# Four moves of vector and scalar work inside the steady step of a four-layer graph kernel

## The chip, the core and the metric

The kernel runs on one core of one Trainium2 chip. A core has five engines with a queue each: TensorE (PE, matmuls), VectorE (DVE, elementwise and reductions), ScalarE (ACT, activations and copies), GpSimd (POOL) and SyncE (SP, which here only issues DMAs). Each engine takes its own queue in order, and semaphores make it wait for another. The metric is device time in microseconds (us), lower is better; the time before is the median of three runs.

## The reference, cut to what matters

The input x is 128 graphs of 64 nodes with 512 features, in float32. Four layers follow one another, each with a residual and a layer norm:

- layer 0: a hypergraph convolution (512 to 1024 features, relu, layer norm over 1024, back to 512), `y + x`, then again `x + ...` and a layer norm;
- layer 1: a score per node, `exp(leaky(8 tanh(s/8)))` times the adjacency, normalised, applied to x and multiplied by `w`;
- layer 2: three graph convolutions, `relu(adj @ (x @ W1) + b1)`, `relu(adj @ (. @ W2) + b2)`, `adj @ (. @ W3) + b3`;
- layer 3: attention with 8 heads, whose probabilities get `LG * adj + LD * exp(-adj)` added under a mask, an output projection and a bias.

Two pieces of algebra matter below. The kernel folds layer 0's inner layer norm into W2: gamma scales W2's rows, and beta times W2 becomes a row `bw_bc` that is added to x, scaled by a column sum `cs` of the graph matrix. And x is doubled and gets b2 before W2's product is added, since layer 0 adds x twice.

## The kernel before, in words

**Tiling.** Two graphs fill the 128 partitions (a pair), four pairs are a group of 512 rows, and there are 16 groups. Every group goes through three parts: `a` (layers 0 and 1, `first_half`), `b` (layer 2 and the queries and keys of layer 3, the first part of `second_half`) and `t` (the rest of layer 3). Step s works on part `a` of group s, part `b` of group s-1 and part `t` of group s-2 at once; steps 2 to 15 are the steady ones, and have one order of pieces (`order`, L1285). Step 1, step 16 and what follows have orders of their own.

**Products.** A 512x512x512 product (`multiply`, L520) is made of seven products of halves instead of eight, in the order B11, T1, T2, B21, T3, B22, T4. They accumulate in three PSUM tiles: `a` takes B11, then T2, T3 and T4 on top; `b` takes T1, then B22; `c` takes B21. Between them the running values are evicted: u1 after B11, u5 after T1, u2 after T2 (`snap`, L525), and the four results after B21, T3, B22 and T4. So T2 can't start before u1 is out of `a`, T3 not before u2, T4 not before the result after T3. The activations' side needs four sums of quarters (`Left.sums`, L488, four VectorE additions); the weights' sums lie in DRAM and are streamed by SP through a ring of 20 tiles. The first and second product of layer 0 are called W1a and W1b here (hidden columns 0 to 511 and 512 to 1023), the third W2 (twice as deep); layer 2's are l2a, l2b and l2c.

**What sets the order of the work.** In the steady steps the program's text gives only a priority: a scheduler at build time places each instruction on its engine's queue. `behind(key)` (L475) keeps instructions behind a named one, which is the eviction after B22 of product `key`. The order on the chip is that of the built program and doesn't change with the data. In a steady step of the program before, it is:

- PE: ... layer 2's aggregation `gt_l` of group s-1, W1a, l2a, W1b with the transposes of the probabilities in it, the attention product `pv` of group s-2, l2b with half of layer 0's `gt_l0h`, the other half, W2 with layer 2's `gth` in it, l2c, ...
- PE twice takes a product apart: W1a's B21 (tile `c_l0w`) runs half before T2 and half after it, and W1b's first product runs a quarter before l2a's T4 and the rest after it.
- DVE, around W1a: the sums of layer 2 (`s_l`, `aT_l`; `left.sums()` at L993), then u1, u5, u2 and the results of W1a, then `doubled` (L791) and `constant` (L797, the column-sum scalings), then the results of l2a.
- ACT: the relu of W1b's two halves of rows (L702; the second is a 128x1024 activation behind the last eviction of W1b), then four copies of the attention product out of PSUM (`aT_oT`, L1275), with a table load and two square roots among them, then u1 of l2b.
- DVE, between l2b's last eviction and W2's first: x plus b3 (`gb3_bc`, L1008), the masks of layer 3 (`prepare_masks`, L654), eight sums for W2.
- SP: the masks of a later group (`mj`, `mr`) are reloaded into buffers that `prepare_masks` has just read, between the weights of l2c.

Of the kernel before, what the change touches and what calls it, by code (L numbers as in the profile page):

```python
# [8 lines left out]
FP = mybir.dt.float32  # L9
U8 = mybir.dt.uint8  # L10
AF = mybir.ActivationFunctionType
# [3 lines left out]
P = 128  # L15
C = 64
D = 512
DH = 1024
HEADS = 8
G = 4  # L20
T = G * P
KD = D // P
Q = 256
# [18 lines left out]
def kernel(  # L42
# [31 lines left out]
    NGRP = NPAIR // G  # L74
# [8 lines left out]
    grp = ctx.enter_context(tc.tile_pool(name="grp", bufs=2))  # L83
# [52 lines left out]
    ten, vec, act = Engine(nc.tensor, PE), Engine(nc.vector, DVE), Engine(nc.scalar, ACT)  # L136
# [288 lines left out]
    def bcast(t, n):  # L425

        return t.unsqueeze(2).to_broadcast([P, n, C])

    def row2(t, c0):

        return t[:, c0 : c0 + Q].unsqueeze(1).to_broadcast([P, 2, Q])
# [38 lines left out]
            act.copy(o[:, :, :, g, :], ps[g])  # L470


    last_add = {}

    def behind(key):  # L475
        return tc.issue_after(last_add[key]) if key in last_add else nullcontext()
# [43 lines left out]
    def multiply(lefts, wt_q, dst, key, flipped=False, res=None, stops=(3,)):  # L520


        acc = [ps_acc.tile([P, 2, Q], FP, name=f"{n}_{key}", tag="acc") for n in "ab"]

        def snap(ps, m, n, what):  # L525
            t = work.tile([P, 2, Q], FP, name=f"{what}_{key}", tag="w")
            if res is None:
                act.copy(t, ps)
            else:
                vec.tensor_add(t, ps, res(m, n))  # L530
            return t

        pa, pc = acc
        product(pa, lefts, wt_q, B11, True, False, flipped)
        s1 = snap(pa, 0, 0, "u1")
        if 1 in stops:
            yield
        product(pc, lefts, wt_q, T1, True, False, flipped)
        s5 = snap(pc, 1, 1, "u5")
        if 2 in stops:  # L540
            yield
        product(pa, lefts, wt_q, T2, False, False, flipped)
        s2 = snap(pa, 0, 1, "u2")
        if 3 in stops:
            yield
        pb = ps_acc.tile([P, 2, Q], FP, name=f"c_{key}", tag="acc")
        product(pb, lefts, wt_q, B21, True, True, flipped)
        vec.tensor_add(dst(0, 0), pb, s1)
        if 4 in stops:
            yield  # L550
        product(pa, lefts, wt_q, T3, False, False, flipped)
        vec.tensor_add(dst(1, 1), pa, s5)  # L552
        if 5 in stops:
            yield
        product(pc, lefts, wt_q, B22, False, True, flipped)
        last_add[key] = vec.tensor_add(dst(0, 1), pc, s2).ins  # L556
        if 6 in stops:
            yield
        product(pa, lefts, wt_q, T4, False, True, flipped)
        if res is None:  # L560
            act.copy(dst(1, 0), pa)
        else:
            vec.tensor_add(dst(1, 0), pa, res(1, 0))
# [9 lines left out]
    def turned(t):  # L573

        return lambda m, n: t[:, 2 * n : 2 * n + 2, m * Q : (m + 1) * Q]
# [78 lines left out]
    def prepare_masks(g):  # L654
        q = g["q"]
        mj, mr = g["mj"], g["mr"]

        neg = grp.tile([P, 2, 2, C], FP, name=f"neg_{q}", tag="neg", bufs=1)
        n3 = neg.rearrange("p a g j -> p (a g) j")
        vec.tensor_mul(  # L660
            n3, mj.rearrange("p a g j -> p (a g) j"), bcast(mi[:, q * G : (q + 1) * G], G)
        )
        vec.tensor_scalar(neg, neg, BIG, BIG, ALU.mult, ALU.subtract)

        m2 = grp.tile([P, G, C], FP, name=f"m2_{q}", tag="m2", bufs=1)
        vec.tensor_mul(m2, mr, bcast(mcol[:, q * G : (q + 1) * G], G))
        adt = grp.tile([P, G, C], FP, name=f"adt_{q}", tag="adt", bufs=1)
        act.activation(adt, g["atc"], AF.Exp, scale=-1.0)
        if LD != LA:
            vec.tensor_scalar_mul(adt, adt, LD / LA)  # L670
        vec.scalar_tensor_tensor(adt, g["atc"], LG / LA, adt, ALU.mult, ALU.add)
        vec.tensor_mul(adt, adt, m2)
        g["neg"], g["adt"] = neg, adt


    def first_half(g):
        q, xg = g["q"], g["x"]
        pair = lambda p: xg[:, p, :]

        left = Left(f"l0_{q}")  # L680
# [4 lines left out]
        h = [big.tile([P, 2, DH], FP, name=f"h_{q}_{m}", tag="big") for m in range(2)]  # L685
        for n in range(2):
            for i, _ in enumerate(multiply(
                [left], (w_1[n], q),
                lambda m, k: h[m][:, :, n * D + k * Q : n * D + (k + 1) * Q],
                f"l0w1{n}_{q}",  # L690
                res=lambda m, k: row2(b1_bc, n * D + k * Q),
                stops=((2, 4), (2, 3))[n] if q == 1 else (3,),
            )):
                yield f"w1{'ab'[n]}{i + 1}"
            yield "w1" + "ab"[n]

            if n == 0:
                st = small.tile([P, G, 2, 6], FP, name=f"sth_{q}", tag="sth", bufs=2)
            with behind(f"l0w1{n}_{q}"):
                for m in range(2):  # L700
                    hn = h[m][:, :, n * D : (n + 1) * D]
                    act.activation(hn, hn, AF.Relu)  # L702
                    for p in range(2):
                        vec.bn_stats(st[:, 2 * m + p, n, :], hn[:, p, :])
            if n == 0:
                if q > 1:
                    with behind(f"l0w10_{q}"):
                        doubled(g)
                        constant(g)
                yield "resid"  # L710
        for m in range(2):
            mv = small.tile([P, 2, 2], FP, name=f"mvh_{q}_{m}", tag="mvh")
# [9 lines left out]
        for duo in range(2):  # L722
            for u in range(2):
                graph_T(
                    lambda p: h[p // 2][:, p % 2, u * D : (u + 1) * D], g["sm"], lefts[u].t, duo, f"l0h{u}_{q}"
                )
            if duo == 0:
                yield "c2a"
        for left in lefts:
            left.sums()  # L730
        yield "c2b"
# [21 lines left out]
        t = grp.tile([P, G, C], FP, name=f"t_{q}", tag="t", bufs=1)  # L753
# [16 lines left out]
        left = Left(f"l1_{q}")  # L770
# [26 lines left out]
    def constant(g):  # L797
        for p in range(G):
            vec.scalar_tensor_tensor(
                g["x"][:, p, :], bw_bc, g["cs"][:, p : p + 1], g["x"][:, p, :], ALU.mult, ALU.add  # L800
            )
# [184 lines left out]
    def second_half(g):  # L986
        q, xg = g["q"], g["x"]
        pair = lambda p: xg[:, p, :]

        left = Left(f"l2_{q}")  # L990
        for duo in range(2):
            graph_T(pair, g["atc"], left.t, duo, f"l2_{q}")
        left.sums()  # L993
        yield "gt"
        h1 = Left(f"h1_{q}")
        for _ in multiply([left], (w_g[0], q), turned(h1.t), f"l2a_{q}", flipped=True):
            yield "l2a1"
# [5 lines left out]
        for _ in multiply([h1], (w_g[1], q), nat(g2), f"l2b_{q}"):  # L1003
            yield "l2b1"
        yield "l2b"
        with behind(f"l2b_{q}"):
            for p in range(G):
                vec.tensor_add(xg[:, p, :], xg[:, p, :], gb3_bc)  # L1008
            prepare_masks(g)
        yield "gb3"  # L1010


# [1 line left out]
        for c2 in range(2):  # L1014
            ps = [ps_gt.tile([P, 2, G, C], FP, name=f"gth2_{q}_{c2}_{h}", tag="gt") for h in range(2)]
            for c in range(2):
                for p in range(G):
                    for f in range(2):
                        for h in range(2):
                            rows, c0 = slice(h * C, (h + 1) * C), (2 * c2 + c) * P + f * C  # L1020
                            ten.matmul(  # L1021
                                ps[h][f * C : (f + 1) * C, c, p, :],
                                g2[rows, p, c0 : c0 + C], g["atc"][rows, p, :], start=True, stop=True,
                            )
            for c in range(2):
                k = 2 * c2 + c
                o = h2.t[:, k, :].rearrange("p (d h t) -> p d h t", d=2, h=2)
                for h in range(2):
                    act.activation(  # L1029
                        o[:, :, h, :], ps[h][:, c].rearrange("p (d a) i -> p d (a i)", d=2),  # L1030
                        AF.Relu, bias=gb2_col[:, k : k + 1],
                    )
        h2.sums()
        yield "gh"
        g3 = big.tile([P, G, D], FP, name=f"g3_{q}", tag="big")
# [3 lines left out]
        for duo in range(2):  # L1039
            ps = [ps_gt.tile([P, D], FP, name=f"agg_{q}_{duo}_{p}", tag="gt") for p in range(2)]  # L1040
# [14 lines left out]
        left = Left(f"xT_{q}")  # L1055

        for duo in range(2):
            ps = [ps_gt.tile([P, KD, 2, C], FP, name=f"xtp_{q}_{duo}_{h}", tag="gt") for h in range(2)]
# [40 lines left out]
        left = Left(f"oT_{q}")  # L1099
# [204 lines left out]
    for what in start:  # L1304
        who, dot, name = what.partition(".")
# [7 lines left out]
    for step in range(1, NGRP + 2):  # L1313
        for what in orders.get(step, order):
            who, dot, name = what.partition(".")
            key = (who, step - lag[who], name) if dot else (what, step + 1, None)
# [24 lines left out]
    for n, (who, q, name) in enumerate(todo):  # L1341
# [28 lines left out]
        elif who == "rest":  # L1370
            with in_turn(SP, POOL):
# [8 lines left out]
                gb3_bc = load_row(gb3, D, "gb3_bc")  # L1380
# [66 lines left out]
```

## Time and profile before

| what | value |
|---|---|
| median of 3 runs | 2797.4 us (2797.36 to 2798.42) |
| the profiled execution | 2797.61 us, its span 2795.8 us, TensorE clock 1.00 |
| PE busy | 2769.4 us (99%) |
| DVE busy | 2000.2 us (72%) |
| ACT busy | 818.3 us (29%) |
| one steady step, from one `dot` to the next | 171.77 us |

The span runs from the first to the last instruction. PE is the engine without room; the others have idle time that costs nothing as long as PE doesn't wait for them. Matmuls are pipelined, and one that is held up looks busy while it is held: the distance between the starts of successive groups tells more than their busy time.

### The profile page before, as it was taken

How to read it: one execution, taken by the hardware profiler on the slowest of the kernel's cores; microseconds unless marked ns; L12 is line 12 of the kernel's file. 1: busy time of each engine (PE TensorE's matmuls, PEld its weight loads, DVE VectorE, ACT ScalarE, POOL GpSimd, SP SyncE). 2: the span in 40 equal slices, each digit the busy share in tenths (PEclk: the TensorE clock that was granted, in tenths of full speed). 3: DMA queues.
4: the chain of work that ended last, by engine and by line, in shares of the span. 5: the costliest groups of instructions: out<-in, count | busy, mean ns of one | idle time of the engine just before them, and what ended most of it. 6: DMA issues, size and time to landing. Idle time of an engine off the chain costs nothing.

```text
span 2795.8 us, 67769 instructions
## 1 busy us (share of the span) xinstructions
PE 2769.4 (99%) x28870; PEld 2362.2 (84%) x28870; DVE 2000.2 (72%) x3858; ACT 818.3 (29%) x1469; POOL 38.1 (1%) x72
## 2 busy tenths in 40 slices
PE   9999999999999999999999999999999999999998
PEld 7878888888888888888888888888888888888887
DVE  6768687676776767767677676767767677676766
ACT  3222323232232223323223222332322323232232
POOL 2000000000000000000000000000000000000000
PEclk9999999999999999999999999999999999999999
DMA  8444455454544545445454454544545455454541
GB/s 255 162 136 145 129 158 145 133 163 130 166 130 140 161 132 166 122 141 165 124 168 130 139 161 136 155 130 143 162 127 163 129 148 152 126 163 127 154 122 61
DMA packets 309389, 405.15 MB, mean 145 GB/s; under 512 B 57409, under 2 KB 185185, under 8 KB 309089
## 3 DMA queue, kind: packets, MB, share of 16 engines
q1 hardware_dynamic: 304112, 385.05, 46.5%
q0 software_dynamic: 4976, 15.76, 1.5%
q8 instruction: 229, 3.75, 0.5%
q14 instruction: 72, 0.58, 0.1%
HBM read 369.78 MB, written 30.93 MB: 143 GB/s over the span
## 4 chain that ended last, share of the span: by engine, by line
PE 86%; DVE 7%; issue 4%; ACT 1%; DMA 1%; POOL 0%; SPq 0%; DVEq 0%; POOLq 0%
PE a_l0w L513 13%; PE b_l0w L513 7%; PE a_l2b L513 4%; PE a_q L513 4%; PE a_k L513 4%; PE a_v L513 4%; PE c_l0w L513 4%; PE a_l2a L513 4%; PE a_l1w L513 4%; PE gt_l L462 3%; PE a_wo L513 3%; PE a_l2c L513 2%; PE gt_l0h L462 2%; PE b_l1w L513 2%; PE b_l2b L513 2%
## 5 line engine op out<-in xcount | busy, mean ns | idle before, releaser
L513 PE MATMUL a_l0w<-w2w,aT_l0h 128*128 128x256 f32 x720 | 164.3, 381 | 0.0
L444 DVE BATCH_NORM_STATS2 st_l<-x 128x6 f32<-128x512 f32 x244 | 157.4, 671 | 0.1
L513 PEld LDWEIGHTS a_l0w<-w2w,aT_l0h 128*128 128x128 f32 x720 | 135.6, 190 | 18.8
L702 ACT ACTIVATE h<-h 128x1024 f32<-128x1024 f32 x58 | 61.3, 1057 | 216.6 <-DVE h L556 195.0
L448 DVE TENSOR_SCALAR x<-x,mv_l,rs_l 128x512 f32<-128x512 f32 x244 | 117.9, 540 | 1.8
L470 ACT COPY aT_l<-gt_l 128x512 f32<-128x512 f32 x176 | 90.4, 600 | 71.6 <-PE gt_l L462 71.5
L513 PE MATMUL b_l0w<-w2w,s_l0h 128*128 128x256 f32 x480 | 108.5, 379 | 0.0
L513 PEld LDWEIGHTS b_l0w<-w2w,s_l0h 128*128 128x128 f32 x480 | 90.1, 190 | 13.5
L1029 ACT ACTIVATE aT_h<-gth,gb_col 128x256 f32<-128x256 f32 x128 | 48.4, 489 | 159.0 <-PE gth L1021 159.0
L435 ACT ACTIVATE rs_l<-mv_l,eps_t 128x4 f32<-128x4 f32 (+1 forms) x64 | 19.0, 297 | 253.7 <-DVE mv_l L445 241.9
L513 PE MATMUL a_l2b<-gwbw,aT_h 128*128 128x256 f32 x360 | 86.6, 383 | 5.4 <-ACT aT_oT L1275 5.4
L513 PE MATMUL a_q<-aT_xT,wqw 128*128 128x256 f32 x360 | 86.6, 383 | 0.7 <-ACT aT_xT L1068 0.7
L513 PE MATMUL a_l2a<-aT_l,gwaw 128*128 128x256 f32 x360 | 86.5, 383 | 0.0
L513 PE MATMUL a_l2c<-gwcw,aT_h 128*128 128x256 f32 x360 | 85.3, 380 | 0.6 <-DVE g L552 0.6
L513 PE MATMUL a_l1w<-ww,aT_l 128*128 128x256 f32 x360 | 85.1, 379 | 0.0
L513 PE MATMUL a_k<-aT_xT,wkw 128*128 128x256 f32 x360 | 85.0, 379 | 0.0
L513 PE MATMUL a_l0w<-w1aw,aT_l 128*128 128x256 f32 x336 | 82.3, 388 | 0.0
L513 PE MATMUL a_l0w<-w1bw,aT_l 128*128 128x256 f32 x336 | 81.7, 379 | 0.0
L530 DVE TENSOR_TENSOR u_l0w<-a_l0w,b_bc 128x512 f32<-128x512 f32 x56 | 38.4, 686 | 59.8 <-PE a_l0w L513 59.8
L513 PE MATMUL a_v<-wvw,aT_xT 128*128 128x256 f32 x336 | 80.8, 383 | 0.0
L513 PEld LDWEIGHTS a_l2b<-gwbw,aT_h 128*128 128x128 f32 x360 | 67.2, 190 | 15.9 <-ACT aT_oT L1275 7.4
L513 PE MATMUL a_wo<-wow,aT_oT 128*128 128x256 f32 x336 | 79.5, 379 | 0.1
(531 smaller groups left out, 6471.1 us busy)
## 6 DMA issues: line engine op xcount, KB each, us to landing
w2w<-w2k SPq DMA_DIRECT2D x210, 256.0 KB, 2.7
x<-in_x_dram SPq DMA_DIRECT2D x15, 1024.0 KB, 6.7
w1aw<-w1ak SPq DMA_DIRECT2D x60, 256.0 KB, 2.7
w1bw<-w1bk SPq DMA_DIRECT2D x60, 256.0 KB, 2.6
ww<-wk SPq DMA_DIRECT2D x60, 256.0 KB, 2.8
gwaw<-gwak SPq DMA_DIRECT2D x60, 256.0 KB, 3.6
gwbw<-gwbk SPq DMA_DIRECT2D x60, 256.0 KB, 2.7
gwcw<-gwck SPq DMA_DIRECT2D x60, 256.0 KB, 2.7
```

The costliest lines, as they stand in the source:

```text
L435: act.activation(rs[:, at], mv[:, at, 1], AF.Sqrt, bias=eps_t)
L444: vec.bn_stats(st, xg[:, p, :])
L448: vec.tensor_scalar(xg[:, p, :], xg[:, p, :], mv[:, p, 0:1], rs[:, p : p + 1], ALU.subtract, ALU.mult)
L462: ten.matmul(ps[g][f * C : (f + 1) * C, c, p, :], src(2 * duo + p)[rows, c0 : c0 + C], mat[rows, 2 * duo + p, :], start=True, stop=True,)
L470: act.copy(o[:, :, :, g, :], ps[g])
L513: ten.matmul(acc[:, blk, :], lhsT, rhs, start=(first and blk == 0 and i == 0), stop=(last and i == n_k - 1), skip_group_check=True,)
L530: vec.tensor_add(t, ps, res(m, n))
L702: act.activation(hn, hn, AF.Relu)
L1029: act.activation(o[:, :, h, :], ps[h][:, c].rearrange("p (d a) i -> p d (a i)", d=2), AF.Relu, bias=gb2_col[:, k : k + 1],)
```

## The change

It moves four things of the steady step and leaves the arithmetic as it is:

1. layer 2's sums go from before W1a's u1 to behind W1a's u2 ("the third eviction");
2. `constant` goes from behind W1a to behind l2b's eviction after B22 of the group before;
3. the addition of b3 and `prepare_masks` go from behind l2b to behind W2's u2;
4. the last relu of W1b is issued in two halves of columns, the half that T3 completes first.

To be able to name u1, u5 and u2, `snap` now notes each in `last_add`. Groups 0 and 15 keep the old place of points 1 and 3 (`alone`), and point 2 holds for groups above 1.

```diff
         def snap(ps, m, n, what):
             t = work.tile([P, 2, Q], FP, name=f"{what}_{key}", tag="w")
-            if res is None:
-                act.copy(t, ps)
-            else:
-                vec.tensor_add(t, ps, res(m, n))
+            last_add[f"{key}.{what}"] = (act.copy(t, ps) if res is None else vec.tensor_add(t, ps, res(m, n))).ins
             return t
...
-        adt = grp.tile([P, G, C], FP, name=f"adt_{q}", tag="adt", bufs=1)
-        act.activation(adt, g["atc"], AF.Exp, scale=-1.0)
+        adt = g["adt"]
...
+    def shifted(g, key):
+
+        with behind(key):
+            for p in range(G):
+                vec.tensor_add(g["x"][:, p, :], g["x"][:, p, :], gb3_bc)
+            prepare_masks(g)
...
                     hn = h[m][:, :, n * D : (n + 1) * D]
+                    if n == 1 and m == 1:
+
+                        act.activation(hn[:, :, Q:], hn[:, :, Q:], AF.Relu)
+                        hn = hn[:, :, :Q]
                     act.activation(hn, hn, AF.Relu)
                     for p in range(2):
-                        vec.bn_stats(st[:, 2 * m + p, n, :], hn[:, p, :])
+                        vec.bn_stats(st[:, 2 * m + p, n, :], h[m][:, p, n * D : (n + 1) * D])
...
                         doubled(g)
-                        constant(g)
...
             if duo == 0:
                 yield "c2a"
+        if q > 1:
+            with behind(f"l2b_{q - 1}"):
+                constant(g)
...
-        left.sums()
+        alone = q == 0 or q == NGRP - 1
+        if alone:
+            left.sums()
         yield "gt"
+        if not alone:
+            with behind(f"l0w10_{q + 1}.u2"):
+                left.sums()
...
-        with behind(f"l2b_{q}"):
-            for p in range(G):
-                vec.tensor_add(xg[:, p, :], xg[:, p, :], gb3_bc)
-            prepare_masks(g)
+        adt = grp.tile([P, G, C], FP, name=f"adt_{q}", tag="adt", bufs=1)
+        act.activation(adt, g["atc"], AF.Exp, scale=-1.0)
+        g["adt"] = adt
+        if alone:
+            shifted(g, f"l2b_{q}")
         yield "gb3"
...
+        if not alone:
+            shifted(g, f"l0w2_{q + 1}.u2")
         h2.sums()
         yield "gh"
```

In the built program the queues of steps 2 to 15 change as follows, and nowhere else except for the relu of step 1. PE: W1a's B21 is in one piece behind T2, and W1b's first product in one piece behind l2a's T4; all else stands as before. DVE: two of layer 2's sums stand behind u2, the result after B21 follows, then the other two; the four `constant` instructions and the nine of b3 and masks change places as described. ACT: one instruction more a step, in the order right half of the second row block, first row block, left half of the second. SP: the four mask loads stand behind the fifth of the seven weight tiles of the output projection, where they stood between the weights of l2c. POOL has no change.

More of the change, by code (lines that the diff above doesn't have):

```diff
@@ L672, in prepare_masks @@
         vec.tensor_mul(adt, adt, m2)
-        g["neg"], g["adt"] = neg, adt
+        g["neg"] = neg
+    def shifted(g, key):
[3 more added lines that the diff above has]
+            prepare_masks(g)
     def first_half(g):
```

## The prediction

> **What bounds the kernel now.** The page first: its head, part 1.
>
> ```profile
> span 2795.8 us, 67769 instructions
> PE 2769.4 (99%) x28870; PEld 2362.2 (84%) x28870; DVE 2000.2 (72%) x3858; ACT 818.3 (29%) x1469; POOL 38.1 (1%) x72
> ```
>
> PE has 26 us without an instruction, and everything else has room. So the change is worth what it takes from PE's own line, and the page can't show that: a matmul that is held up counts as busy. PE's waits, second, name one steady wait, 15 times; the rest of that list is single waits, most at the start.
>
> ```profile
> PE a_l2b L513 <- ACT aT_oT L1275: 5.4, 15, 0.7
> ```
>
> Third, the timeline of PE in one steady step (1172 to 1350 us; start, length, what). I read the starts. Undisturbed, eight 128x256 matmuls take 1.726 us: the five products of l2a from 1311.46 to 1320.09 take 8.63.
>
> ```profile
> 1300.68 1.89 PE L513 MATMUL b_l0w<-w1aw,s_l 128*128 128x256 f32 x8
> 1302.40 1.03 PE L513 MATMUL c_l0w<-w1aw,aT_l 128*128 128x256 f32 x4
> 1303.40 1.99 PE L513 MATMUL a_l0w<-w1aw,s_l 128*128 128x256 f32 x8
> 1305.23 1.03 PE L513 MATMUL c_l0w<-w1aw,aT_l 128*128 128x256 f32 x4
> 1306.17 1.99 PE L513 MATMUL a_l0w<-w1aw,aT_l 128*128 128x256 f32 x8
> 1308.01 1.89 PE L513 MATMUL b_l0w<-w1aw,s_l 128*128 128x256 f32 x8
> ...
> 1320.09 1.89 PE L513 MATMUL b_l2a<-s_l,gwaw 128*128 128x256 f32 x8
> 1321.82 0.59 PE L513 MATMUL a_l0w<-w1bw,aT_l 128*128 128x256 f32 x2
> 1322.36 1.99 PE L513 MATMUL a_l2a<-aT_l,gwaw 128*128 128x256 f32 x8
> 1324.19 1.46 PE L513 MATMUL a_l0w<-w1bw,aT_l 128*128 128x256 f32 x6
> 1325.48 1.89 PE L513 MATMUL b_l0w<-w1bw,s_l 128*128 128x256 f32 x8
> ...
> 1337.29 2.10 PE L1266 MATMUL pv<-pt,v 64*64 64x64 f32 x128
> 1339.71 1.99 PE L513 MATMUL a_l2b<-gwbw,aT_h 128*128 128x256 f32 x8 [0.33 <-ACT aT_oT L1275]
> ```
>
> Three places lose time. W1a: 1300.68 to 1308.01 is 7.33 us for four products (T1, B21, T2, T3), which is 0.42 over 4 x 1.726 = 6.90. W1b: 1320.09 to 1325.48 is 5.39 us for three (l2a's B22 and T4, W1b's first), 0.21 over 5.18. Attention: `pv` to `a_l2b` is 2.42 us, where another run of 128 small matmuls (`dot`, 1280.29 to 1282.32) takes 2.03: 0.39. A fourth place follows: `b_l2b` at 1341.54, its T2 at 1343.44 and the next run at 1345.36, 0.17 + 0.1 lost.
>
> Fourth, who is late there. DVE and ACT, same window:
>
> ```profile
> 1302.66 0.68 DVE L530 TENSOR_TENSOR u_l0w<-a_l0w,b_bc 128x512 f32<-128x512 f32 x1
> 1318.37 2.73 DVE L799 SCALAR_TENSOR_TENSOR x<-bw_bc,cs,x 128x512 f32<-128x512 f32 x4
> 1321.62 0.68 DVE L552 TENSOR_TENSOR aT_h<-a_l2a,u_l2a 128x512 f32<-128x512 f32 x1
> 1201.09 0.69 DVE L548 TENSOR_TENSOR x<-c_l0w,u_l0w 128x512 f32<-128x512 f32 x1 [4.98 <-PE c_l0w L513]
> ```
>
> ```profile
> 1338.12 1.06 ACT L702 ACTIVATE h<-h 128x1024 f32<-128x1024 f32 x1 [0.67 <-DVE h L563]
> 1339.08 1.06 ACT L1275 ACTIVATE aT_oT<-pv 128x512 f32<-128x512 f32 x2
> ```
>
> u1 of W1a ends at 1303.34, and T2 starts 0.06 later; layer 2's sums (1300.12 to 1302.66) are ahead of u1. `constant` holds l2a's evictions, so the one after T3 ends at 1322.30 and T4 starts at 1322.36. The last relu holds the first `aT_oT` copy, which ends near 1339.66; `a_l2b` takes that PSUM buffer and starts at 1339.71. Each PE start sits on the end of the very work that the change moves.
>
> **What the Trainium skill says.** "TensorE: Matmul & The Clock Gate", Step-by-step, has matmuls stay in program order, so one that waits holds all behind it; the trace agrees, as the three places push everything later. "Perfetto Trace Analysis", Identifying the Most-Contended Engine, says matmul busy is a poor measure of distance to the limit; here the step has 171.38 busy of 171.77 us, and over 1 us of it is lost. "ScalarE: Activation LUTs", What ACT_TABLE_LOAD costs, prices an activation with immediate scale and bias at 186 ns + 0.833 ns per element and an overlap of 93 ns: 1039 ns for 1024 elements, where the trace has 1057, and 613 ns for 512, where the exponentials of that size (L1188) take 627.
>
> **The change part by part**, laid out from the starts above.
>
> *Sums behind u2.* B11 ends at about 1300.88 (its last matmul's start plus 0.38 and 0.04 to DVE). u1 runs 1300.88 to 1301.57, and T2, due at 1302.40, needs no filler. u5 at 1302.6. T2 ends in results at 1304.33: u2 to 1305.02, before T3 is due at 1305.86. Then the queue has two sums, the result after B21, two sums, the result after T3: 0.60 each and 0.73 behind a dependence puts the last at 1308.07 to 1308.76; T4 is due at 1309.31. Margin 0.55. l2a's T1 needs the first sum from 1312.8, long done. Gain 0.42, bounds 0 (if T4 waits) and 0.42.
>
> *Constant behind l2b.* Without 2.73 us in its way the result after l2a's B21 is taken as it comes, that after T3 by 1320.6 (all now 0.42 earlier) and T4 is due at 1321.40: 0.8 of margin. Gain 0.21, bounds 0 and 0.21; W1b follows 0.63 earlier. At its new place `constant` takes 2.73 us where b3 and masks took 4.07 (1181.71 to 1185.78), so W2's sums come up to 0.8 sooner. Cost nothing: W2's B11 (3.5 us) runs meanwhile, and without that cover it would still be 1.3 less than before.
>
> *b3 and masks inside W2.* 4.07 us behind u2 (1195.41 to 1196.1) end near 1200.2; DVE's next work comes at 1201.09, out of the idle 4.98 in the row above. Cost 0, cover 0.9; overrun would delay the result after B21, and PE only once the result after T3 (taken at 1204.54, needed by T4 at 1207.80) begins 2.6 late. b3 is wanted at `agg`, 1233; the masks at `dot`, 80 us on; the exponential stays where it was in ACT's queue. On SP four mask loads wait for the mask work, now until about 1199, and end by 1202 (3.2 us from release to end before). Behind them stand two of the output projection's weight tiles, issued at 1200.22 and 1201.08 before, now some 2 us later; the first is used at 1237.68, and such a load lands 2.7 us after issue. Nothing.
>
> *Relu in two parts.* The right half runs while B22's result is awaited. Behind the last eviction only 512 elements are left: 0.63 in place of 1.06. ACT's relu began 0.73 after that eviction's start, 1337.39; both 0.63 earlier now, so it runs 1337.49 to 1338.12, the copy (0.1 overlap) 1338.02 to 1338.60, and `a_l2b` could start at 1338.65. PE brings it at 1339.31 - 0.63 = 1338.68. Gain 0.40 (0.39 by the rows, 0.403 by single starts). Bounds: 0 (if the half costs as much as the whole) and 0.40. The extra instruction, about 0.1 of ACT, lies in its idle time. The fourth place stays: from the first copy to u1 ACT works without a pause (1339.08 to 1343.38, 4.30), so u1 ends at 1342.32, and T2 is due at 1342.24. Taken as 0; bounds 0 and 0.27.
>
> *Sum.* 0.42 + 0.21 + 0.40 = 1.03 us a step. Steps 2 to 15 have all three, 14 x 1.03 = 14.4 us; step 1's relu has no PE wait behind it. The span goes 2795.8 to 2781.4, its execution 2797.61 to 2783.2, and the median, 0.2 below that execution, to 2783.0.
>
> **The rivals.**
> - *One of the three stays.* A margin of 0.03 (relu) or 0.55 (T4) is eaten: 2785.9 without W1b's part, 2788.7 without the relu's or W1a's, 2786 with half of one. For it: the relu's margin is thin; against: it fails gradually, 0.05 late costs 0.05.
> - *The fourth place goes too.* If u1 comes 0.1 earlier than laid out: 14 x 0.27 = 3.8 more, 2779.2.
> - *The time returns elsewhere*, the step being set by weights: 2797. Against: SP's loads are issued some 30 us ahead, DMA is under half busy, DVE idles at every place used.
> - *Slower.* The four sums now stand between W1a's u2 and the result after T3. Past the margin of 0.55 each us late is a us of PE, plus 0.1 for starting again; at 1.9 us late a step loses 1.45, more than 0.4 over what it gains, and ends above 2803. The sums took 2.54 us before and would have to take 4.4; I see nothing that stretches them.
>
> **How the numbers follow.** The forecast 0.77, by itself 2781.5 to 2784.5; one stays 0.12; the fourth goes 0.05; returned 0.03; slower 0.03. The range, 2780 to 2788, takes most of the second and the edge of the third. Less than 0.2% (5.6 us) can't be told from no change. Faster 0.94, same 0.03, slower 0.03.
>
> **What would show it.** In the profile after: a step of 170.74 us instead of 171.77; no wait of `a_l2b` on `aT_oT` outside step 16; W1a's four products 6.90 us apart, in one piece each; l2a's T4 1.73 after its B22; T2 of l2b still late by 0.17. Wrong it would be if T4 of W1a, or W2's T4, starts on the end of a DVE eviction, or if `a_l2b` still starts on the end of the copy, later than 2.1 us after W1b's last eviction began (2.32 before, 1.92 laid out).

## The result and the profile after

| | before | changed |
|---|---|---|
| median | 2797.12 us (2796.25 to 2798.42, 6 runs) | 2782.74 us (2781.63 to 2785.03, 6 runs) |
| ratio, 95% interval | | 0.995, 0.9938 to 0.9961 |
| profiled execution, its span | 2797.61, 2795.8 us | 2783.17, 2781.4 us |
| steady step, `dot` to `dot` | 171.765 us | 170.70 us |

The change is faster by 0.5%; 2783.0 us was forecast. The head of the page and two lines of PE's waits of the changed kernel (us in total, times, longest):

```profile
span 2781.4 us, 67713 instructions
PE 2758.2 (99%) x28870; PEld 2366.0 (85%) x28870; DVE 2002.3 (72%) x3858; ACT 819.7 (29%) x1484; POOL 38.1 (1%) x72
```

```profile
PE gt_l L462 <- issue: 1.1, 1, 1.1
PE a_l2b L514 <- ACT aT_oT L1293: 0.7, 1, 0.7
```

PE has as many matmuls as before and is busy for 11.2 us less: the time that went was held-up matmuls, not work. The wait on `aT_oT` that came 15 times comes once, in step 16. (Numbers of lines move: the products' L513 is L514, `aT_oT`'s L1275 is L1293.)

PE's timeline of the step that was shown of before (start, length, what; this run's clock is some 7 us ahead there):

```profile
1294.48 1.89 PE L514 MATMUL b_l0w<-w1aw,s_l 128*128 128x256 f32 x8
1296.20 1.89 PE L514 MATMUL a_l0w<-w1aw,s_l 128*128 128x256 f32 x8
1297.93 1.89 PE L514 MATMUL c_l0w<-w1aw,aT_l 128*128 128x256 f32 x8
1299.66 1.89 PE L514 MATMUL a_l0w<-w1aw,aT_l 128*128 128x256 f32 x8
1301.38 1.89 PE L514 MATMUL b_l0w<-w1aw,s_l 128*128 128x256 f32 x8
1303.11 1.89 PE L514 MATMUL a_l0w<-w1aw,aT_l 128*128 128x256 f32 x8
...
1313.47 1.89 PE L514 MATMUL b_l2a<-s_l,gwaw 128*128 128x256 f32 x8
1315.20 1.89 PE L514 MATMUL a_l2a<-aT_l,gwaw 128*128 128x256 f32 x8
1316.92 1.89 PE L514 MATMUL a_l0w<-w1bw,aT_l 128*128 128x256 f32 x8
...
1330.45 2.10 PE L1284 MATMUL pv<-pt,v 64*64 64x64 f32 x128
1332.48 1.99 PE L514 MATMUL a_l2b<-gwbw,aT_h 128*128 128x256 f32 x8
1334.31 1.89 PE L514 MATMUL b_l2b<-gwbw,s_h 128*128 128x256 f32 x8
1336.18 1.99 PE L514 MATMUL a_l2b<-gwbw,s_h 128*128 128x256 f32 x8
```

W1a's four products from T1 to T3 take 6.90 us (1294.48 to 1301.38; before 7.33), every one in one piece. l2a's T4 follows its B22 by 1.73. `pv` to `a_l2b` is 2.03 (before 2.42). The last pair is the place that was to stay: `b_l2b` to its T2 is 1.87 where 1.73 would be undisturbed.

DVE and ACT of the changed kernel around the same places (in brackets the idle time ahead of the instruction, and what ended it):

```profile
1298.13 0.69 DVE L528 TENSOR_TENSOR u_l0w<-a_l0w,b_bc 128x512 f32<-128x512 f32 x1 [1.03 <-PE a_l0w L514]
...
1301.87 0.68 DVE L550 TENSOR_TENSOR h<-a_l0w,u_l0w 128x512 f32<-128x512 f32 x1
...
1313.74 0.69 DVE L550 TENSOR_TENSOR aT_h<-a_l2a,u_l2a 128x512 f32<-128x512 f32 x1 [1.04 <-PE a_l2a L514]
...
1365.60 0.69 DVE L546 TENSOR_TENSOR x<-c_l0w,u_l0w 128x512 f32<-128x512 f32 x1 [0.91 <-PE c_l0w L514]
```

```profile
1331.28 0.63 ACT L710 ACTIVATE h<-h 128x512 f32<-128x512 f32 x1 [0.67 <-DVE h L561]
1331.82 1.06 ACT L1293 ACTIVATE aT_oT<-pv 128x512 f32<-128x512 f32 x2
1332.90 1.28 ACT L435 ACT_TABLE_LOAD   x1
...
1335.54 0.58 ACT L528 COPY u_l2b<-a_l2b 128x512 f32<-128x512 f32 x1
```

W1a's result after T3 is taken at 1301.87 and T4 starts at 1303.11; l2a's is taken as it comes; behind b3 and masks inside W2 DVE still idles for 0.91 us before the next result. Only 0.63 us of relu stand ahead of the `aT_oT` copies.

### The profile page after: what moved, and what is told of

Its sections match the earlier page's. It is cut to its first block, busy times and chain, and to the rows that moved or that the text cites. A ratio compares the mean times of both kernels' runs of the same rounds, so it can differ in the third digit from the quotient of the medians.

```text
span 2781.4 us, 67713 instructions
## 1 busy us (share of the span) xinstructions
PE 2758.2 (99%) x28870; PEld 2366.0 (85%) x28870; DVE 2002.3 (72%) x3858; ACT 819.7 (29%) x1484; POOL 38.1 (1%) x72
## 4 chain that ended last, share of the span: by engine, by line
PE 87%; DVE 7%; ACT 0%; issue 0%; DMA 0%; DVEq 0%
PE a_l0w L514 13%; PE b_l0w L514 7%; PE a_l2b L514 4%; PE a_q L514 4%; PE a_k L514 4%; PE a_v L514 4%; PE c_l0w L514 4%; PE a_l1w L514 4%; PE a_l2a L514 4%; PE gt_l L462 3%; PE a_wo L514 3%; PE a_l2c L514 2%; PE gt_l0h L462 2%; PE b_l1w L514 2%; PE b_q L514 2%; PE b_k L514 2%
## 5 line engine op out<-in xcount | busy, mean ns | idle before, releaser
L514 PE MATMUL a_l0w<-w2w,aT_l0h 128*128 128x256 f32 x720 | 164.3, 381 | 0.0
L514 PEld LDWEIGHTS a_l0w<-w2w,aT_l0h 128*128 128x128 f32 x720 | 135.6, 190 | 18.8
L514 PE MATMUL b_l0w<-w2w,s_l0h 128*128 128x256 f32 x480 | 108.5, 379 | 0.0
L710 ACT ACTIVATE h<-h 128x1024 f32<-128x1024 f32 (+1 forms) x58 | 54.9, 947 | 178.5 <-DVE h L554 157.5
L514 PEld LDWEIGHTS b_l0w<-w2w,s_l0h 128*128 128x128 f32 x480 | 91.1, 190 | 12.5
L514 PE MATMUL a_l2b<-gwbw,aT_h 128*128 128x256 f32 x360 | 86.6, 383 | 0.7 <-ACT aT_oT L1293 0.7
L514 PE MATMUL a_q<-aT_xT,wqw 128*128 128x256 f32 x360 | 86.6, 383 | 0.7 <-ACT aT_xT L1086 0.7
L514 PE MATMUL a_l2c<-gwcw,aT_h 128*128 128x256 f32 x360 | 85.3, 380 | 0.6 <-DVE g L550 0.6
L514 PE MATMUL a_l1w<-ww,aT_l 128*128 128x256 f32 x360 | 85.1, 379 | 0.0
L514 PE MATMUL a_l2a<-aT_l,gwaw 128*128 128x256 f32 x360 | 85.0, 379 | 0.0
L514 PE MATMUL a_k<-aT_xT,wkw 128*128 128x256 f32 x360 | 85.0, 379 | 0.0
L514 PE MATMUL a_l0w<-w1aw,aT_l 128*128 128x256 f32 x336 | 80.8, 383 | 0.0
L514 PE MATMUL a_v<-wvw,aT_xT 128*128 128x256 f32 x336 | 80.8, 383 | 0.0
L514 PE MATMUL a_wo<-wow,aT_oT 128*128 128x256 f32 x336 | 79.5, 379 | 0.1
L514 PE MATMUL a_l0w<-w1bw,aT_l 128*128 128x256 f32 x336 | 79.4, 379 | 0.0
L514 PEld LDWEIGHTS a_q<-aT_xT,wqw 128*128 128x128 f32 x360 | 67.2, 190 | 14.2 <-DVE qT L550 4.8
```

The costliest lines, as they stand in the source:

```text
L514: ten.matmul(acc[:, blk, :], lhsT, rhs, start=(first and blk == 0 and i == 0), stop=(last and i == n_k - 1), skip_group_check=True,)
```

## The experiments

The theory is the prediction's: three waits of PE, one for each of parts 1, 2 and 4, part 3 costing nothing. Its rivals are that one wait stands in for another, that the order of PE's products itself costs time, and that margins are thinner than laid out. For each run the step is given too, since it shows hundredths that the median doesn't. "Single starts" are the trace's starts of single matmuls, which the timeline merges into rows; undisturbed they lie 216 ns apart for 128x256.

### Part 1 alone

```diff
...
-        left.sums()
+        alone = q == 0 or q == NGRP - 1
+        if alone:
+            left.sums()
         yield "gt"
+        if not alone:
+            with behind(f"l0w10_{q + 1}.u2"):
+                left.sums()
```

> The kernel before with the first part alone (layer 2's four sums behind W1a's third eviction). Theory of the prediction: only W1a's lost 0.42 us a step comes back; the constant still stands ahead of layer 2's evictions (0.21) and the last relu still holds the transposed copy (0.40). 14 steady steps x 0.42 = 5.9 us less than before: 2791.3 us, a step of 171.35 us, W1a whole, the distance from pv to a_l2b still 0.55 us. Rival (the sums only change which wait comes last, another takes its place): within 1 us of before. Rival (the T3 eviction becomes late behind the sums): 1 to 2 us a step slower, 2811 to 2825.

Measured: 2792.23 us, ratio 0.998 (0.9972 to 0.9987); step 171.355, so 0.41 us less. W1a is whole, and from the last matmul of `pv` to the first of `a_l2b` the single starts are 551 ns apart, as before. The theory holds; no other wait took the place of this one. The built program of this run takes u1 out earlier and joins W1a's B21 at once; which of the two gave what is asked under "The order of W1a's products".

### Part 4 alone

```diff
+                    if n == 1 and m == 1:
+                        act.activation(hn[:, :, Q:], hn[:, :, Q:], AF.Relu)
+                        hn = hn[:, :, :Q]
                     act.activation(hn, hn, AF.Relu)
...
```

> The kernel before with the fourth part alone (the last relu in two halves). Theory: the first copy of the transposed heads is no longer held, pv to a_l2b 0.15 us in place of 0.55, 14 x 0.40 = 5.6 us: 2791.6 us. Rival (the 0.40 is only pushed on to the second place, where layer l2b waits for its u1 on ScalarE, which is bound by the same chain of copies and table load): within 1 us of before, the wait ahead of l2b's T2 longer by 0.40 a step.

Measured: 2791.39 us, ratio 0.9978 (0.9969 to 0.9986); step 171.35, 0.415 us less. From the last matmul of `pv` to the first of `a_l2b` 148 ns in place of 551. The wait at l2b's T2 didn't grow: from 383 to 357 ns between the two single starts, it shrank. The rival falls.

### Part 2 alone

```diff
                         doubled(g)
-                        constant(g)
...
+        if q > 1:
+            with behind(f"l2b_{q - 1}"):
+                constant(g)
```

> The kernel before with the second part alone (the constant's scalings behind layer l2b's last eviction, masks where they were). Theory that the parts need each other: shift, masks and constant now lie in one stretch of VectorE between l2b's last eviction and the copies and sums of W2, so W2's first products start late: about 0.85 and then 1.1 us a step, less the 0.21 that the constant's old place gives back, so about 1.75 x 14 = 24 us slower, 2821 us. Rival (the parts are independent, VectorE has the room): 14 x 0.21 = 2.9 us faster, 2794.2 us.

Measured: 2820.51 us, ratio 1.0082 (1.0067 to 1.0097); step 173.44, 1.68 us more. DVE and PE of this kernel, in the same step:

```profile
1362.91 2.73 DVE L801 SCALAR_TENSOR_TENSOR x<-bw_bc,cs,x 128x512 f32<-128x512 f32 x4
1365.56 1.89 DVE L1010 TENSOR_TENSOR x<-x,gb_bc 128x512 f32<-128x512 f32 x3
1367.37 0.68 DVE L492 TENSOR_TENSOR s_l0h<-aT_l0h 128x512 f32<-128x512 f32 x1
```

```profile
1369.50 1.03 PE L513 MATMUL b_l0w<-w2w,s_l0h 128*128 128x256 f32 x4
1371.11 2.86 PE L513 MATMUL b_l0w<-w2w,s_l0h 128*128 128x256 f32 x12 [0.58 <-DVE s_l0h L492]
1374.73 3.72 PE L513 MATMUL a_l0w<-w2w,s_l0h 128*128 128x256 f32 x16 [0.76 <-DVE u_l0w L530]
```

`constant` and the additions of b3 fill DVE until W2's sums; the masks run between those. T1 of W2 stops after a quarter for its sums, and T2 waits for u1, which is queued behind it all. T1 to T2 is 5.23 us here and 3.46 in the changed kernel. So part 2 is worth 0.2 us a step only where part 3 has made room; by itself it costs eight times as much.

### Part 3 alone, and parts 2 and 3

The edit is `shifted` with its two calls, as in the change; for the second run the edit above is added.

```diff
-        with behind(f"l2b_{q}"):
-            for p in range(G):
-                vec.tensor_add(xg[:, p, :], xg[:, p, :], gb3_bc)
-            prepare_masks(g)
...
+        if not alone:
+            shifted(g, f"l0w2_{q + 1}.u2")
         h2.sums()
```

> The kernel before with the third part alone (shift and masks inside W2, the constant still ahead of layer 2's evictions). Theory: the masks were hidden behind l2b and stay hidden inside W2, the step stays at 171.77 us and the time within 1 us of before (ratio 0.9996 to 1.0004). Rival (W2's evictions have no room for about 5 us of masks without a cost): 0.2 us or more a step, 2800 us or more.

> The kernel before with the second and third part (constant behind l2b, shift and masks inside W2). Theory: the constant's 0.21 us a step comes back and the masks cost nothing inside W2: 14 x 0.21 = 2.9 us less, 2794.2 us. Rival (masks inside W2 delay W2's evictions): 0.3 us or more a step the other way, 2798 us or more.

Measured: part 3 alone 2798.13 us, ratio 1.0003 (0.9994 to 1.0012), step 171.77. Parts 2 and 3 2795.05 us, ratio 0.9991 (0.9982 to 0.9999), step 171.565, 0.20 us less; W1b's first product and l2a's T4 are whole there. Both as the theory has it: part 3 is free and gives nothing, and it is what lets part 2 give its 0.20. W1b's first product, which the kernel before cuts around l2a's T4, wasn't cut again by itself; in the kernel before the single starts at its two joins are 216 ns apart, so nothing was lost there but the wait of T4.

The steps of the single parts give 0.41 + 0.20 + 0.415 = 1.03 us; together the change gives 1.065. By the single starts the waits that the change takes away add up to that: 0.42 (W1a) + 0.21 (l2a's T4) + 0.40 (`a_l2b`) + 0.03 (l2b's T2). In the runs of part 1, of part 4 and of parts 2 and 3 about 0.01 each comes back, a few ns at a time, mostly at the waits of q's T4 and of the column sums `ss`, which are treated below.

### The order of W1a's products, kept split

The changed kernel, with B21 of W1a halved around T2 again.

```diff
...
+            with in_turn(PE):
+                ws = product(pb, lefts, wt_q, B21, True, True, flipped, (0,))
+            with in_turn(PE):
+                product(pa, lefts, wt_q, T2, False, False, flipped)
+            s2 = snap(pa, 0, 1, "u2")
+            with in_turn(PE):
+                product(pb, lefts, wt_q, B21, True, True, flipped, (1,), ws)
...
```

> The changed kernel with W1a's B21 on TensorE in two halves again, one ahead of T2 and one behind it, as the kernel before had it; the sums stay behind the third eviction. Theory of the prediction (the lost 0.42 us were a wait for u1, the order of the products itself costs nothing): the step stays at 170.70 us, 2782.7 us. Rival (cutting the product in two costs by itself, by loading weights again or by restarting): 0.2 to 0.4 us a step more, 2785.5 to 2788.5 us.

Measured: 2785.06 us, ratio to before 0.9951 (0.9936 to 0.9966), an interval that the changed kernel's own overlaps; but the step is 170.89 us in all regular steps, 0.19 us more. The rival's size is right, and not its reason. PE and DVE of this kernel:

```profile
1297.64 1.89 PE L515 MATMUL a_l0w<-w1aw,s_l 128*128 128x256 f32 x8
1299.36 1.03 PE L515 MATMUL c_l0w<-w1aw,aT_l 128*128 128x256 f32 x4
1300.31 1.99 PE L515 MATMUL a_l0w<-w1aw,aT_l 128*128 128x256 f32 x8
```

```profile
1299.57 0.69 DVE L531 TENSOR_TENSOR u_l0w<-a_l0w,b_bc 128x512 f32<-128x512 f32 x1 [1.90 <-PE a_l0w L515]
```

T2 is due and starts on time: nothing is lost at the cut itself, where the starts are 216 ns apart as anywhere. But behind T2 only half of B21 is left, 0.86 us, and u2 comes into PE's way: it begins 0.21 us after T3's cover did, and T3 starts 0.74 after that. T3's first matmul is 84 ns late and its second 104 more. With B21 whole behind T2 there is 1.73 us of cover.

u2 of the kernel before, whose T3 starts at 1306.17, again 0.74 after it:

```profile
1305.43 0.69 DVE L530 TENSOR_TENSOR u_l0w<-a_l0w,b_bc 128x512 f32<-128x512 f32 x1 [1.49 <-PE a_l0w L513]
```

Since the kernel before has the same two figures at T3 (+83 and +104 ns) and others at T2 (+127 and +104), its lost 0.42 is two waits: 0.23 at T2 for u1, held by the sums, and 0.19 at T3 for u2, which no sum held. The second came from the order of PE, and went because the built program no longer cut B21.

### The margin behind the sums

```diff
...
+        if key.startswith("l0w10_") and int(key[6:]) > 1:
+            for _ in range(2):
+                with in_turn(DVE):
+                    vec.tensor_add(spare, wa_bc, bw_bc)
+            with in_turn(DVE):
+                vec.tensor_add(dst(1, 1), pa, s5)
...
```

> The changed kernel with two useless additions of 128x512 (0.60 us each on VectorE) ahead of W1a's third eviction, and the last of layer 2's four sums behind it, so that the eviction slips by 0.60 us net. Theory (the eviction leaves its buffer 0.56 us before T4 wants it): T4 is late by 0.05 us and pays 0.10 us for the restart, 0.15 us a step, 14 x 0.15 = 2.1 us, 2784.8 us. Rival (there is no margin, and the gain hung on the place of the sums to the last tenth): 0.7 us a step, 2792.5 us. Rival (the margin is wider than the trace shows): 2782.7 us.

Measured: 2785.81 us, ratio to before 0.9954 (0.9939 to 0.9969); step 170.905, 0.205 us more.

```profile
1300.26 1.89 PE L516 MATMUL a_l0w<-w1aw,aT_l 128*128 128x256 f32 x8
1301.99 1.89 PE L516 MATMUL b_l0w<-w1aw,s_l 128*128 128x256 f32 x8
1303.81 1.99 PE L516 MATMUL a_l0w<-w1aw,aT_l 128*128 128x256 f32 x8
```

```profile
1303.08 0.68 DVE L557 TENSOR_TENSOR h<-a_l0w,u_l0w 128x512 f32<-128x512 f32 x1
```

The eviction begins 2.82 us after T3's start; in the changed kernel it was 2.21. T4 starts 0.73 after it. So there the buffer was free at 2.94 and wanted at 3.45: the margin is 0.51 us. The 0.61 us of slip less 0.51 is the 0.10 by which T4 is late (312 ns to the start before, 216 undisturbed), and the second matmul adds 0.10. The theory holds, with its margin of 0.56 too wide by 0.05.

### What is left: three waits of the changed kernel

In the changed kernel's single starts three places of a steady step still lose time. ACT's table load between the `aT_oT` copies makes u1 of l2b late (142 + 104 ns); four scalings of a layer norm stand ahead of q's results on DVE (about 108 + 104 ns); and row sums for a later group stand ahead of the operand `e` of the column sums `ss` (216 + 104 ns). Each was moved by itself, and then all three.

The table, fetched by an activation of one column whose result isn't used:

```diff
+                    if n == 1 and m == 0 and q > 1:
+                        early = small.tile([P, 1], FP, name=f"early_{q}", tag="early")
+                        act.activation(early, h[1][:, 0, D + Q : D + Q + 1], AF.Sqrt, bias=eps_t, scale=0.0)
```

> The changed kernel with the square root's table fetched on ScalarE ahead of the relus, by a one-column activation whose result nobody reads, so that the 1.28 us load no longer lies between the copies of the transposed heads. Theory: u1 of layer l2b leaves ScalarE at about 1335.8 in place of 1336.1 us on the clock of the changed kernel, T2 of l2b starts on time: 0.14 + 0.10 us a step, 14 x 0.25 = 3.4 us, 2779.3 us. Rival (the load merely moves the stall to the relus, which are due 0.03 us after they come): 0.3 us or more a step slower, 2787 us.

Measured: 2779.34 us, ratio to before 0.9931 (0.9916 to 0.9946); step 170.455, 0.245 less.

```profile
1325.25 1.28 ACT L708 ACT_TABLE_LOAD   x1
...
1334.31 0.59 ACT L528 COPY u_l2b<-a_l2b 128x512 f32<-128x512 f32 x1
```

The load lies in ACT's idle time behind the exponential of the masks, and u1 begins 0.88 us after `b_l2b` (1333.43 there), where it was 1.23 (1334.31 and 1335.54 above). T2 starts 216 ns behind the matmul before it.

The scalings, behind q's result after T3:

```diff
...
-        layer_norm(xg, f"l1_{q}")
+        scaled = layer_norm(xg, f"l1_{q}", after=q if q > 1 else None)
         yield "p2"
+        if q > 1:
+            with behind(f"q_{q - 1}.r3"):
+                scaled()
+        yield "p3"
...
```

The lines left out make `layer_norm` give back its scalings as `scaled`, and put `p3` behind `q` in the order of pieces.

> The changed kernel with the four scalings of the next layer norm on VectorE behind the third eviction of q. Theory: q's T4 no longer waits for that eviction (0.11 us) nor restarts (0.10 us), and nothing wants the scaled rows before: 14 x 0.21 = 3.0 us, 2779.7 us. Rival (the scaled rows are then late for the layer's graph products): 0.2 us or more a step slower, 2785.5 us or more.

Measured: 2779.62 us, ratio to before 0.9932 (0.9916 to 0.9949); step 170.495, 0.205 less. First the changed kernel's DVE and its T4 of q, then those of this one:

```profile
1255.67 1.92 DVE L448 TENSOR_SCALAR x<-x,mv_l,rs_l 128x512 f32<-128x512 f32 x4
1257.51 0.68 DVE L546 TENSOR_TENSOR qT<-c_q,u_q 128x512 f32<-128x512 f32 x1
1258.11 0.68 DVE L550 TENSOR_TENSOR qT<-a_q,u_q 128x512 f32<-128x512 f32 x1
```

```profile
1257.01 1.89 PE L514 MATMUL b_q<-s_xT,wqw 128*128 128x256 f32 x8
1258.84 1.99 PE L514 MATMUL a_q<-aT_xT,wqw 128*128 128x256 f32 x8
```

```profile
1255.84 0.69 DVE L556 TENSOR_TENSOR qT<-a_q,u_q 128x512 f32<-128x512 f32 x1 [0.99 <-PE a_q L520]
1256.44 1.45 DVE L450 TENSOR_SCALAR x<-x,mv_l,rs_l 128x512 f32<-128x512 f32 x3
```

```profile
1255.64 1.89 PE L520 MATMUL b_q<-s_xT,wqw 128*128 128x256 f32 x8
1257.36 1.89 PE L520 MATMUL a_q<-aT_xT,wqw 128*128 128x256 f32 x8
```

T4 started 0.73 after the result's eviction did, at 1.83 us from B22; now the eviction runs as B22 begins, and T4 follows at 1.72.

The row sums, behind the last product of layer 1's weights:

```diff
-        ... load a.w21 b.gh a.w2 rows b.l2c1 b.l2c2 a.ss b.l2c t.o1 a.den t.o2 ...
+        ... load a.w21 b.gh a.w2 b.l2c1 b.l2c2 a.ss b.l2c t.o1 a.den rows t.o2 ...
...
-            with behind(f"l0w2_{q - 1}" if q > 2 else "q_0") if q > 1 else nullcontext():
+            with behind(f"den_{q - 1}" if q > 2 else "q_0") if q > 1 else nullcontext():
```

> The changed kernel with the row sums of the next group's adjacency, on VectorE and its loads on SP, behind the sums and the reciprocal of layer 1 in place of ahead of them. Theory: the operand of the column sums is written earlier, TensorE no longer waits for it (0.22 us) nor restarts (0.10 us), 13 x 0.32 = 4.1 us, 2778.6 us, a step of 170.38 us. Rival (the row sums are then late for the next step, or the late loads are): 0.3 us or more a step the other way, 2787 us or more.

Measured: 2780.28 us, ratio to before 0.9938 (0.9923 to 0.9952); step 170.47, 0.23 less where 0.32 was expected. The wait of 216 ns is gone in every steady step. Of the 104 behind it some 76 came back (the second `ss` starts 240 to 247 ns after the first), but the second matmul of the `a_l2c` run that follows (l2c's T3) is now 49 to 55 ns late: 216 + 76 - 52 = 240. First the changed kernel's `e` and `ss`, then what this one has, with l2c's u2 and T3:

```profile
1213.44 0.41 DVE L755 TENSOR_TENSOR e<-identc,s 128x256 f32<-128x256 f32 x1
1213.90 0.70 PE L759 MATMUL ss<-e,bones 128*128 128x256 f32 x2
```

```profile
1211.06 0.41 DVE L755 TENSOR_TENSOR e<-identc,s 128x256 f32<-128x256 f32 x1
1211.61 0.62 PE L759 MATMUL ss<-e,bones 128*128 128x256 f32 x2
1211.81 0.59 ACT L528 COPY u_l2c<-a_l2c 128x512 f32<-128x512 f32 x1 [4.59 <-PE a_l2c L514]
1212.50 1.94 PE L514 MATMUL a_l2c<-gwcw,aT_h 128*128 128x256 f32 x8
```

What is left at `ss` is still `e`: in both kernels the second `ss` starts 0.37 us after the end of `e`, in the changed one with the first late (1214.22 after 1213.85), here with the first on time (1211.85 after 1211.47). The 52 ns at T3 fit u2 in the same way: u2 ends at 1212.39, 0.10 before T3 starts, and T3's second matmul comes at 1212.77, 0.37 after it. In the changed kernel the wait at `ss` had put T3 0.40 behind the end of u2, and its second matmul is on time. So the gain of 0.32 was cut by two operands that come just before they are due. No run moves u2 to test that.

All three together:

> The changed kernel with all three: the table fetched early, the layer norm's scalings behind q's third eviction, the row sums behind layer 1. Theory: the three waits lie at different places of the step and come back together, 0.245 + 0.205 as measured alone and 0.32 as estimated: 170.70 - 0.77 = 169.93 us a step, 2782.7 - 14 x 0.45 - 13 x 0.32 = 2772.2 us. Rival (the scalings and the row sums, both moved later on VectorE, meet in the next stage): only two of three come back, 2775 to 2778 us.

Its edit is the three above in one kernel. Measured: 2772.10 us (2771.38 to 2772.59), ratio to before 0.9908 (0.9894 to 0.9923); step 170.01, which is 0.69 less than the changed kernel's and the sum of the three (0.245 + 0.205 + 0.23 = 0.68). The three waits are independent, and with the row sums the same 0.05 at l2c's T3 comes along. The forecast of 2772.2 met the time although the row sums gave 0.09 a step less than it counted, 1.2 us in 13 steps: this run's step from the second `dot` to the third took 170.26 us, where the changed kernel's took 172.13. This is the fastest version here, 10.6 us below the changed kernel's median; the runs of the kernel before beside the two had medians of 2797.22 and 2797.12 us.

## Why the prediction was right

**Bound and method.** PE set the time, and the sum over starts gave the size. Right: 14 steps x 1.03 = 14.4 us were forecast off the span, and 14.4 came off. That it agrees to the tenth is chance. The regular step gained 1.065, so 14.9 in 14 steps; 1.26 more came before the first `dot`; and two irregular steps (172.13 and 171.20, where before had one of 171.97) took 1.7 back. The 1.26 can't be put down to the change: the first `dot` comes at 247.35 us in the changed kernel and at 248.44 in the one with the early table, which has all four parts too and differs from it only in later steps. The 1.1 us wait of `gt_l` on "issue" lies in the first of the irregular steps. Nearly all kernels with changed order have such a longer step from the second `dot` to the third, from 0.25 to 1.9 us over their others; neither the kernel before, nor part 3 alone, nor the one with the margin has it there, but the last has one of 1.3 us, at `gt_l` too, seven steps later. Each kernel has one traced execution; the cause stays open.

**Sums behind u2.** Gain 0.42: right (part 1 alone, 0.41). Two terms were off. The margin of 0.55 counted to the eviction's end and left out the 0.04 from there to PE's start, which the same working used elsewhere: it is 0.51. And the step "each PE start sits on the end of the very work that the change moves" fails for T3: that one waited for u2, which isn't moved, and for 0.19 of the 0.42. It was lost to the cut of B21. Had the cut stayed, the gain would have been 0.23 here and the time 14 x 0.19 = 2.7 us more. So the size was right because the built program joined B21 in the same change, which the prediction laid out but did not count as a cause.

**Constant behind l2b.** Gain 0.21 (0.20), margin 0.8 (0.73: taken at 1313.74, out 0.73 later, T4 at 1315.20). "Cost nothing" at the new place is right because 4.07 us of masks leave that place; with the masks still there it costs 1.68 net.

**b3 and masks inside W2.** Cost 0, cover 0.9: measured 0.91 and a ratio of 1.0003. The late weight tiles were harmless as said: the two behind the mask loads are issued at 1365.89 and 1366.52, 1.2 and 0.9 us later in the step than before, where some 2 were expected, and land 2.9 us after that; the first of them is used at 1402.2.

**Relu in two parts.** Gain 0.40 (403 ns by the single starts), the half at 0.63, `a_l2b` at 1.92 us after W1b's last eviction began (1330.56 to 1332.48): all as laid out. The estimate for 512 elements from the Trainium skill, "ScalarE: Activation LUTs", What ACT_TABLE_LOAD costs, was 613 ns; the trace has 0.63 us.

**The fourth place.** Taken as 0, bounds 0 and 0.27; it gave 0.026 (383 to 357 ns). That is the margin of 0.03 by which ACT came earlier than PE after the relu: ACT's chain moved a little further than PE's start, and u1 at its end with it. Part 4 alone shows the same figure, so it belongs to the relu.

**Rivals.** None of the waits stayed or moved elsewhere. The slower one needed the sums to be 1.9 us late; the margin's run shows that the rule behind it (each us past the margin is a us of PE, and 0.1 for starting again) holds for the first tenth.

## What to carry to other kernels

Where a full engine has no idle time in the page, read the distance between the starts of its groups: a place that exceeds the undisturbed distance is a wait, and the engine whose instruction ends just there names the cause. A product that is cut to fill a gap has less cover behind the gap, so ask for each half what it must cover. When instructions move to a place that is already full, take out first what fills it: the same move was worth +0.2 us or -1.7 us a step.

## What was not expected of the hardware

- Each of these waits of PE cost more than its length: after a delayed start the second matmul came 320 ns after the first instead of 216. It was 104 ns whether the first was late by 84 (T3 in the cut order), 96 (the margin) or 216 ns (`ss`), and also where no wait is seen but a run of 64-wide matmuls ends, as at `a_l2b` behind `pv` (148, then 320). Taking a wait of 0.1 away so gave 0.2.
- A part of the 104 ns can come without a visible wait. In the run of the row sums the first matmul of `ss` and of l2c's T3 started on time, and the second still came 0.37 us after the end of the instruction whose result or buffer the first one needed. The waits that are seen have the same distance (T3 of the kernel before: u2 ends at 1306.12, the second matmul comes at 1306.49). With 0.22 between two matmuls that asks at these places for 0.16 us between that end and the time at which the matmul is due, and not for the 0.05 that a first start shows. By this reading, an estimate that no run was made to test, W1a's T4 had 0.41 us to spare and not 0.51, and a slip of 0.61 should cost 0.20; 0.205 was measured.
- Waits of 0.08 to 0.22 us at a matmul have no line in the list of waits, though they come every step: the places that were worth 0.42 and 0.21 us a step don't stand there, and neither does any of the three that gave the next 0.69.
